# Routing of three mixture-of-experts layers on one Trainium2 core: prefix sums by scan, one-hot rows in halves on VectorE, and some work ordered behind the routing

## Chip, cores and metric

The kernel runs on one core of one Trainium2 chip. The metric is the device time of one execution in microseconds. One core has five engines that run side by side, each in its own fixed order of instructions: TensorE (PE, matmuls; its weight loads are listed as PEld), VectorE (DVE), ScalarE (ACT), GpSimd (POOL) and SyncE (SP, here used for DMA issues). They wait for each other by semaphores. The program is built by a framework whose scheduler chooses the order of each engine's instructions when the kernel is compiled, from the program order, the data dependences and a model of times; an instruction's place in the source is therefore not its place on the engine.

## The reference

The input x is 2 sequences of 1024 tokens with 128 features. Four layers follow, each of the form

```python
xn = layernorm(x)
s = mixer(xn)
g = silu(ffn(xn))
x = x + s * g
```

| layer | mixer | ffn |
|---|---|---|
| 0 | state space (Mamba 2) | 8 experts, the 2 best mixed, computed densely |
| 1 | delta rule (q, k, v, beta; a scan over tokens) | 8 experts, the 2 best, and a shared expert |
| 2 | linear attention, 16 heads | softmax attention, then 8 experts, the 2 best |
| 3 | two state spaces, one forward and one backward | 16 experts, the 2 best, and a shared expert |

The ffn of layer 1 shows what routing has to compute:

```python
logits = xf @ router_w.T + experts_bias
rw, sel = jax.lax.top_k(logits, 2)
rw = softmax(rw)
cw = (one_hot(sel, E) * rw[..., None]).sum(axis=1)
eo = silu(xf @ w1) * (xf @ w3)          # per expert
moe_out = einsum('te,teh,ehd->td', cw, eo, w2)
return moe_out + shared_out
```

## The kernel before

Tokens lie in 16 tiles of 128 (one token to a partition), in 4 groups of 4 tiles. Layers 1 to 3 do not compute every expert for every token. Each of the 2 × 2048 choices gets a slot in a list that is sorted by expert, and the list is cut into blocks of rows of one expert: 39 blocks of 128 rows in layer 1, 23 of 256 in layer 2, 47 of 128 in layer 3. A block gathers its tokens' rows (POOL, indirect DMA, `Dispatch.load`, L1231), loads its expert's weights (SP reads the expert's number from `dof` and issues a DMA, `Dispatch.weights`, L1237), runs the expert, and scatters its rows to the choices' places (POOL, `Dispatch.store`, L1241). At the end `Dispatch.fetch` (L1252) reads the two rows of each token back, and they are weighted and added.

What stands before the first block is the routing:

- `Kern.top2` (L357 to L378) finds the largest and second largest logit of each token, as two one-hot tiles (`rhot`) of 16 tiles × E experts, and the two values (`rm`).
- `Dispatch.__init__` (L1135 to L1227) adds the two one-hots (`dbo`, L1149), and two matmuls with a triangle and with ones (`pr`) give, for each expert, the number of earlier choices within the tile and the tile's total. A ladder over the 16 tiles (a copy and an addition for shifts of 1, 2, 4 and 8; L1159, L1160) makes running totals; `dmo` and `dbl` count each expert's blocks; a ladder over the experts (L1173, L1174) gives the block at which each expert ends (`de`); `dpl` is each choice's slot, and `do` and `dat` (L1185, L1186) pick it for the two choices of each token.
- The slot is split into a block row number and a place in 128 (`dhi`, `dlo`, L1188 to L1195). To turn "slot of a choice" into "choice of a slot", 32 matmuls (`pinv`, one for each tile and choice) multiply a one-hot of the place (`dla`, L1213, eight pieces of four tiles, two buffers) with a one-hot of the row, weighted with the choice's number (`dhh`: the equality on DVE at L1205, the multiply by the number on POOL at L1206). Their sum gives `dto` (L1218, where a row is scattered to) and `dfrom` (L1219, which token is gathered).
- `dpa`, `dex` and `dof` (L1223 to L1227) compare the block numbers with `de` and give each block's expert.
- `pair_softmax` (L379 to L389) makes the two weights of each token (`rd`, `rw`); its Exp runs on ACT.

What runs beside it differs by layer. In layer 1 (L786 to L1003) it is the delta rule. `delta(g, side)` inverts a triangular matrix of four tiles in seven rounds (`Lm` L909, then `pU`, a copy to `U` L284, `pTT`, `TT` L930, `pT`, `T` L937: products on PE, each answered by DVE); two groups run side by side. The program order is: the first two groups' `delta`, all blocks two by two (`block`, L791: transpose `pxb` into `xbT`, products `pgb` and `pub`, `hb` = silu times, product `pob`), four steps of `scan` (products `pWS`, `pO`, `pS`), the other two groups' `delta` (which begins with `pk`), `close`, four more steps, `close`, the shared expert (`shared`, L838: `pgt`, `put`, `po`), then `fetch` and the layer's last operations. In layer 2 (loop from L1076) it is the linear attention (`qg`, `sig`, `qk`) and the blocks (`pxb`, `p`, `po`). In layer 3 (L1722 to L1817) it is the state spaces: the step sizes start from `pdt` (L1726), go through `steps` (L436: `vdtr`, then `softplus`, L341 to L354, sixteen short operations, then `vdA`, L444), and are used by the products `pc` and, through `uda` (L556), `pd`; the matmuls `px` and `pz` belong to the state spaces too. Blocks go four by four there (`pxb`, L1771).

Every plain matmul of the program is issued at L287, inside `Kern.mm`, so the profile's rows are told apart by the names of their tiles.

Of the kernel before, what the change touches and what calls it, by code (L numbers as in the profile page):

```python
# [19 lines left out]
P = 128  # L20
# [252 lines left out]
class Kern:  # L273
# [83 lines left out]
    def top2(self, pool, lg, E):  # L357


        nc = self.nc  # L360
        big = [P, NT, E]
        rev = self.c[f"rev{E}"].unsqueeze(1).to_broadcast(big)
        cur, found = lg, []
        for n in range(2):
            t = lambda s, w: pool.tile(w, F32, name=f"r{s}{n}", tag=f"r{s}{n}")
            m, hot, at = t("m", [P, NT]), t("hot", big), t("at", [P, NT])
            nc.vector.tensor_reduce(m, cur, AX.X, ALU.max)
            nc.vector.tensor_tensor(hot, cur, m.unsqueeze(2).to_broadcast(big), ALU.is_equal)
            nc.vector.tensor_mul(hot, hot, rev)
            nc.vector.tensor_reduce(at, hot, AX.X, ALU.max)  # L370
            nc.vector.tensor_tensor(hot, hot, at.unsqueeze(2).to_broadcast(big), ALU.is_equal)
            found.append((m, hot))
            if n == 0:
                rest = pool.tile(big, F32, name="rrest", tag="rrest")
                nc.vector.scalar_tensor_tensor(rest, hot, -3e38, cur, ALU.mult, ALU.add)
                cur = rest
        return found

    def pair_softmax(self, pool, m1, m2):  # L379

        nc = self.nc
        d = pool.tile([P, NT], F32, name="rd", tag="rd")
        w = pool.tile([P, NT], F32, name="rw", tag="rw")
        nc.vector.tensor_sub(d, m2, m1)
        nc.scalar.activation(d, d, AF.Exp)
        nc.vector.tensor_scalar_add(w, d, 1.0)
        nc.vector.reciprocal(w, w)
        nc.vector.tensor_mul(d, d, w)
        return w, d  # L389
# [275 lines left out]
def layer0(K, x, xn, xT, w, e):  # L665
    nc, tc, c = K.nc, K.tc, K.c
    with ExitStack() as es:
# [49 lines left out]
        (m1, _), (m2, _) = K.top2(pf, lg, 8)  # L717
# [52 lines left out]
def layer1(K, x, xn, xT, w, inp):  # L770
    nc, tc, c = K.nc, K.tc, K.c
    four = [P, G, P]
    with ExitStack() as es:
# [7 lines left out]
        with tc.tile_pool(name="r1", bufs=1) as pr:  # L781
            (m1, h1), (m2, h2) = K.top2(pr, K.logits(pr, sf, xT, w["wr"], w["br"], 8), 8)
            d = Dispatch(K, pf, pr, sf, h1, h2, 8, P, inp["lists"])
            w12 = K.pair_softmax(pf, m1, m2)
# [220 lines left out]
def layer2(K, x, xn, xT, w, inp):  # L1005
# [3 lines left out]
    with ExitStack() as es:  # L1009
# [59 lines left out]
        with ExitStack() as e2:  # L1069
# [7 lines left out]
            with tc.tile_pool(name="r2", bufs=1) as pr:  # L1077
                (m1, h1), (m2, h2) = K.top2(pr, lg, 8)
                d = Dispatch(K, pf, pr, sf, h1, h2, 8, 2 * P, inp["lists"])
                w12 = K.pair_softmax(pf, m1, m2)  # L1080
# [48 lines left out]
class Dispatch:  # L1129
# [5 lines left out]
    def __init__(self, K, keep, pool, ps, h1, h2, E, R, lists, room=None):  # L1135
# [7 lines left out]
        big = [P, NT, E]  # L1143
        flat = lambda a: a.rearrange("p a b -> p (a b)")
        tile = lambda n, shape, dt=F32: pool.tile(shape, dt, name="d" + n, tag="d" + n)
        lt, ones, both = tile("lt", [P, P], F32R), tile("on", [P, P], F32R), tile("bo", big, F32R)
        nc.vector.tensor_copy(lt, c["lt"])
        nc.vector.tensor_copy(ones, c["ones"])
        nc.vector.tensor_add(both, h1, h2)  # L1149

        pr = ps.tile([P, 2, NT, E], F32, name="pr", tag="ps")
        K.mm(flat(pr[:, 0]), lt, flat(both))
        K.mm(flat(pr[:, 1]), ones, flat(both))
        tot = tile("to", big)
        nc.vector.tensor_copy(tot, pr[:, 1])
        cur = tot
        for n, k in enumerate((1, 2, 4, 8)):
            new = tile(f"c{n}", big)
            nc.vector.tensor_copy(new[:, :k, :], cur[:, :k, :])  # L1159
            nc.vector.tensor_add(new[:, k:, :], cur[:, k:, :], cur[:, : NT - k, :])  # L1160
            cur = new
        total = cur[:, NT - 1, :]
# [4 lines left out]
        nc.vector.tensor_tensor(more, total.unsqueeze(2).to_broadcast(shape), marks.unsqueeze(1).to_broadcast(shape), ALU.is_gt)  # L1167
        blocks = tile("bl", [P, E])
        nc.vector.tensor_reduce(blocks, more, AX.X, ALU.add)
        end, k = blocks, 1  # L1170
        while k < E:
            new = tile(f"e{k}", [P, E])
            nc.vector.tensor_copy(new[:, :k], end[:, :k])  # L1173
            nc.vector.tensor_add(new[:, k:], end[:, k:], end[:, : E - k])  # L1174
            end, k = new, 2 * k
        first = tile("fi", [P, E])
        nc.vector.tensor_sub(first, end, blocks)
        place = tile("pl", big)
        nc.vector.tensor_sub(place, cur, tot)
        nc.vector.tensor_add(place, place, pr[:, 0])  # L1180
        nc.vector.scalar_tensor_tensor(place, first.unsqueeze(1).to_broadcast(big), float(R), place, ALU.mult, ALU.add)
        at = tile("at", [P, 2, NT])
        for k, hot in enumerate((h1, h2)):
            one = tile(f"o{k}", big)
            nc.vector.tensor_mul(one, hot, place)  # L1185
            nc.vector.tensor_reduce(at[:, k, :], one, AX.X, ALU.add)  # L1186
# [11 lines left out]
        (where, tag, bufs, most), (there, its, both) = room or ((pool, "dhh", 1, T), (pool, "dla", 2))  # L1198
        per = min(2 * NT, most // wide)
        hot = []  # L1200
        for a in range(0, 2 * NT, per):
            at = slice(a, min(a + per, 2 * NT))
            shape = [P, at.stop - a, wide]
            h = where.tile(shape, F32R, name="dhh", tag=tag, bufs=bufs)
            nc.vector.tensor_tensor(h, c["count"][:, :wide].unsqueeze(1).to_broadcast(shape), digits[0][:, at].unsqueeze(2).to_broadcast(shape), ALU.is_equal)  # L1205
            nc.gpsimd.tensor_mul(h, h.bitcast(F32), c["slot"][:, at].unsqueeze(2).to_broadcast(shape))  # L1206
            hot.append(h)
        pi = ps.tile([P, wide], F32, name="pinv", tag="ps")
        some = 4
        for a in range(0, 2 * NT, some):  # L1210
            shape = [P, some, P]
            lane = there.tile(shape, F32R, name="dla", tag=its, bufs=both)
            nc.vector.tensor_tensor(lane, c["lane"].unsqueeze(1).to_broadcast(shape), digits[1][:, a : a + some].unsqueeze(2).to_broadcast(shape), ALU.is_equal)  # L1213
            for q in range(some):
                K.mm(pi, lane[:, q, :], hot[(a + q) // per][:, (a + q) % per, :], a + q == 0, a + q == 2 * NT - 1)
# [7 lines left out]
        nc.vector.tensor_tensor(past, c["count"][:, : self.n].unsqueeze(2).to_broadcast(shape), end.unsqueeze(1).to_broadcast(shape), ALU.is_ge)  # L1223
# [435 lines left out]
def layer3(K, x, xn, xT, w, inp, out):  # L1659
    nc, tc, c = K.nc, K.tc, K.c  # L1660
    four = [P, G, P]
    with ExitStack() as es:
# [59 lines left out]
        with tc.tile_pool(name="r3", bufs=1) as pr:  # L1722
            lg = pr.tile([P, NT, 16], F32, name="lg")
            nc.vector.tensor_add(lg, pl[:, :, :16], w["br"].unsqueeze(1).to_broadcast([P, NT, 16]))
            pdt = pa.tile([P, NT, 4], F32, name="pdt")
            nc.vector.tensor_mul(pdt, pl[:, :, 16:], rs.unsqueeze(2).to_broadcast([P, NT, 4]))  # L1726
            (m1, h1), (m2, h2) = K.top2(pr, lg, 16)
            d = Dispatch(K, pf, pr, sf, h1, h2, 16, P, inp["lists"], ((pa, "uxs", 4, 1536), (pa, "uda", 2)))
            w12 = K.pair_softmax(pf, m1, m2)
# [137 lines left out]
```

## Time and profile before

| what | us |
|---|---|
| four runs | 1359.48, 1359.87, 1367.20, 1368.66 |
| their median | 1363.53 |
| the profiled execution | 1365.47 |
| its span | 1363.7 |
| mean granted clock of TensorE in it | 0.886 of full speed |

Over the span PE is busy for 1135.2 us, DVE for 876.4, ACT for 634.2 and POOL for 429.8. The three routings lie at these places of the profiled execution (start of the operation named):

| | layer 1 | layer 2 | layer 3 |
|---|---|---|---|
| `dbo` (the two one-hots added) | 263.50 | 871.55 | 1149.72 |
| `dto` of L1155 (totals read from `pr`) | 266.95 | 874.03 | 1151.41 |
| `dof` (the blocks' experts) | 277.55 | 890.09 | 1159.38 |
| `dhh`, equality on DVE | 282.07 | 891.53 | 1160.90 |
| `dhh`, multiply on POOL, its duration | 2.65 | 2.95 | 3.14 |
| the two `dla` beside it, together | 3.43 | 3.75 | 3.85 |
| first `pinv` | 290.99 | 898.11 | 1165.93 |
| `dfrom` | 304.60 | 906.03 | 1175.68 |
| first gather of a block's rows | 305.81 | 907.00 | 1176.13 |
| first `pxb` | 308.67 | 909.61 | 1183.40 |

A row of the timeline has the start, the duration, the engine, the line, the operation, the tile written and the tiles read, with their sizes; in brackets stands how long the engine was idle before it, and what ended that. A row with a count holds several instructions one after the other. Rows of a table by stretches have the engines' busy time in that stretch, the granted clock and the share of the DMA engines.

### The profile page before, as it was taken

Reading aid. Unit: us, or ns where it says so; the run is one execution under the profiler, and the core shown is the slowest. Engines: PE = TensorE matmul, PEld = TensorE weight load, DVE = VectorE, ACT = ScalarE, POOL = GpSimd, SP = SyncE. Lnnn points to the kernel's source line nnn. Section 1 sums busy time; section 2 is a strip of 40 time slices with the busy share of each in tenths; the row PEclk is TensorE's granted clock in tenths of the full one; section 3 lists DMA queues with packets and bytes.
Section 4 is the critical chain, followed back from the end, with each engine's and each line's share of the span. In section 5 each row is a group of like instructions: output and inputs, shape, how many; then the busy total and the mean of one; then the engine's idle time right before and its main releaser. Section 6 shows DMA issues by size and latency. Waiting matters only on the chain. (4 is left out here: it accounts for less than half of the span.)

```text
span 1363.7 us, 19123 instructions
## 1 busy us (share of the span) xinstructions
PE 1135.2 (83%) x6813; PEld 791.6 (58%) x6813; DVE 876.4 (64%) x2169; ACT 634.2 (47%) x1051; POOL 429.8 (32%) x424
## 2 busy tenths in 40 slices
PE   5699875888899738999998998669999918799985
PEld 2367464788799415544444542347778815577664
DVE  6535534785664686677777761987766469566456
ACT  7664934404612332354555666234352316355661
POOL 0352152017555260000000000034766521467743
PEclk9798776889899957799999989869999967699997
DMA  2000003014345200000000000023344530233411
GB/s 90 0 0 1 1 0 130 8 47 139 119 127 161 62 0 0 1 1 1 1 1 16 1 9 1 8 91 102 124 125 140 151 105 24 70 86 99 77 53 47
DMA packets 49039, 75.71 MB, mean 56 GB/s; under 512 B 7335, under 2 KB 36402, under 8 KB 48688
## 3 DMA queue, kind: packets, MB, share of 16 engines
q1 hardware_dynamic: 39632, 54.30, 12.9%
q0 software_dynamic: 8448, 14.98, 4.8%
q10 hardware_dynamic: 864, 5.21, 1.1%
q8 instruction: 54, 0.88, 0.3%
q14 instruction: 41, 0.34, 0.1%
HBM read 63.95 MB, written 12.85 MB: 56 GB/s over the span
## 5 line engine op out<-in xcount | busy, mean ns | idle before, releaser
L1458 DVE TENSOR_REDUCE mx<-pm 128x1 f32<-128x512 f32 (+3 forms) x304 | 182.0, 657 | 65.1 <-PE pm L287 62.8
L1502 ACT ACTIVATE pr<-psc 128x1024 f32<-128x1024 f32 x144 | 139.7, 1022 | 94.7 <-PE psc L287 61.2
L1231 POOL DMA_INDIRECT xb<-xs,dfrom x132 | 132.1, 1000 | 122.5 <-PE pxb L808 28.7
L1241 POOL DMA_INDIRECT ys<-yb,dto x132 | 135.6, 1027 | 79.3 <-issue 30.0
L1206 POOL TENSOR_TENSOR dhh<-dhh,w_c 128x1280 fp32r<-128x1280 f32 (+2 forms) x3 | 8.7, 2915 | 473.4 <-DVE dhh L1205 473.4
L287 PE MATMUL pm<-kT,qT 32*128 32x128 f32 (+3 forms) x576 | 118.9, 365 | 16.4 <-DVE mx L1458 12.5
L287 PEld LDWEIGHTS pm<-kT,qT 32*128 32x128 f32 x576 | 69.1, 203 | 69.0 <-DVE mx L1458 49.2
L287 PE MATMUL p<-xbT,tw 128*128 128x256 f32 x368 | 101.9, 395 | 3.9 <-ACT sg L1112 2.4
L1112 ACT ACTIVATE sg<-p,tw 128x256 f32<-128x256 f32 x92 | 41.1, 474 | 97.2 <-PE p L287 91.8
L287 PE MATMUL pat<-pr,va 128*32 128x512 f32 x576 | 82.1, 637 | 0.2 <-ACT pr L1502 0.2
L293 PE MATMUL tp<-w_c,xn 128*128 128x128 f32 x64 | 19.5, 419 | 71.2 <-DVE xn L328 43.9
L287 PEld LDWEIGHTS p<-xbT,tw 128*128 128x128 f32 x368 | 64.2, 196 | 14.2 <-ACT sg L1112 3.9
L1113 DVE SCALAR_TENSOR_TENSOR hh<-p,tw,sg 128x256 f32<-128x256 f32 x92 | 42.5, 478 | 38.5 <-ACT sg L1112 32.3
L287 PE MATMUL psc<-qT,kT 32*128 32x512 f32 x288 | 63.9, 488 | 3.4 <-ACT pr L1502 3.2
L287 PEld LDWEIGHTS po<-tw,hh 128*128 128x128 f32 x368 | 54.3, 192 | 8.1 <-issue 2.2
L293 PEld LDWEIGHTS tp<-w_c,xn 128*128 128x128 f32 x64 | 11.8, 191 | 78.9 <-DVE xn L328 27.8
L287 PE MATMUL po<-tw,hh 128*128 128x128 f32 x368 | 56.1, 276 | 0.8 <-DVE hh L1113 0.4
L287 PE MATMUL psc<-mT,onesR 32*128 32x512 f32 x288 | 53.7, 413 | 0.0
L282 ACT COPY xbT<-pxb 128x256 f32<-128x256 f32 (+3 forms) x39 | 15.6, 400 | 64.8 <-PE pxb L808 45.2
L287 PEld LDWEIGHTS psc<-qT,kT 32*128 32x128 f32 x288 | 30.2, 188 | 16.5 <-ACT pr L1502 14.3
L287 PE MATMUL pd<-uda,w_c 128*128 128x512 f32 x64 | 36.5, 674 | 0.9 <-ACT usz L528 0.9
L556 POOL TENSOR_TENSOR uda<-w_c,vdA 128x512 f32<-128x512 f32 x20 | 21.1, 1066 | 50.7 <-PE pd L287 50.0
(529 smaller groups left out, 2833.2 us busy)
## 6 DMA issues: line engine op xcount, KB each, us to landing
tw<-in_rows SPq DMA_DIRECT2D x23, 836.0 KB, 4.6
tw<-in_rows SPq DMA_DIRECT2D x39, 384.0 KB, 3.3
yt<-ys SPq DMA_DIRECT2D x24, 256.0 KB, 3.3
tw<-in_rows SPq DMA_DIRECT2D x47, 128.0 KB, 2.2
xb<-xs,dfrom POOLq DMA_INDIRECT x132, 3.4
ys<-yb,dto POOLq DMA_INDIRECT x132, 2.5
xs<-xn SPq DMA_DIRECT2D x8, 256.0 KB, 2.3
w_l<-in_l ACTq DMA_DIRECT2D x1, 1890.0 KB, 11.1
```

Of the source, the lines that this page charges most:

```text
L282: self.nc.scalar.copy(out, in_)
L287: self.nc.tensor.matmul(out, lhsT=lhsT, rhs=rhs, start=start, stop=stop)
L293: self.nc.tensor.transpose(pt[:, j, :], src(g * G + j), self.c["ident"])
L556: pool.tensor_mul(da, upto.unsqueeze(1).unsqueeze(1).to_broadcast(lay), m["dA"][:, i0 + j : i0 + j + per, :].unsqueeze(3).to_broadcast(lay))
L1112: nc.scalar.activation(sg, p1[:, k - k0, :], AF.Silu, bias=t[:, 1536 + k : 1537 + k])
L1113: nc.vector.scalar_tensor_tensor(hh[:, k, :], p2[:, k - k0, :], t[:, 1540 + k : 1541 + k], sg, ALU.add, ALU.mult)
L1206: nc.gpsimd.tensor_mul(h, h.bitcast(F32), c["slot"][:, at].unsqueeze(2).to_broadcast(shape))
L1231: self.K.nc.gpsimd.indirect_dma_start(dst, None, self.xs, bass.IndirectOffsetOnAxis(self.of_token[:, n : n + 1], 0))
L1241: d = self.K.nc.gpsimd.indirect_dma_start(self.ys, bass.IndirectOffsetOnAxis(self.to[:, n : n + 1], 0), src, None, bounds_check=2 * T - 1, ...
L1458: nc.vector.tensor_reduce(mx[:, starts.index(a), g, j : j + k], tile[0][:, : k * m].rearrange("p (j m) -> p j m", m=m), AX.X, ALU.max)
L1502: K.nc.scalar.activation(pr, ps, AF.Exp, scale=scale)
```

## The change

1. `top2` keeps its two one-hots in one tile of 2 × 16 × E and returns it whole.
2. In `Dispatch.__init__` the sums are laid out with the experts outside and the tiles inside. The ladder over tiles becomes one scan over all experts' tiles (state × mask + total; the mask, `fresh`, is 0 at each expert's first tile and 1 elsewhere, written by two memsets on POOL); its data come straight from `pr`. The ladder over experts becomes a scan of 8 or 16 numbers. The triangle is now the negative of another constant, so that one addition where there were a subtraction and an addition gives the place. The two products and sums over experts become one of twice the size.
3. The one-hot rows `dhh` are written in two halves of 16 tiles; equality and multiply are both on DVE, each half just ahead (in the program's order) of the lanes that use it.
4. `behind` adds an order, without a semaphore, for the scheduler: one instruction is to stand after another of the same engine. The blocks' experts (`past`, so `dof`), the first operation of `pair_softmax` and, in layer 3, `pdt` are put behind the last `dla`.

```diff
+    def behind(self, op, first):
+        self.tc.add_manual_dep(op.ins, first.ins.name, mybir.DependencyInfo(mybir.DependencyClass.NoSync, mybir.DependencyReason.SCHED_ONLY), reason="order")
...
-    def pair_softmax(self, pool, m1, m2):
+    def pair_softmax(self, pool, m1, m2, first):
...
-        nc.vector.tensor_sub(d, m2, m1)
+        self.behind(nc.vector.tensor_sub(d, m2, m1), first)
...
-        nc.vector.tensor_copy(lt, c["lt"])
+        nc.vector.tensor_scalar_mul(less, c["ge"], -1.0)
...
-        tot = tile("to", big)
-        nc.vector.tensor_copy(tot, pr[:, 1])
-        cur = tot
-        for n, k in enumerate((1, 2, 4, 8)):
-            new = tile(f"c{n}", big)
-            nc.vector.tensor_copy(new[:, :k, :], cur[:, :k, :])
-            nc.vector.tensor_add(new[:, k:, :], cur[:, k:, :], cur[:, : NT - k, :])
-            cur = new
+        fresh = tile("fr", big)
+        nc.gpsimd.memset(fresh, 1.0)
+        nc.gpsimd.memset(fresh[:, :, 0], 0.0)
+        cur = tile("cu", big)
+        nc.vector.tensor_tensor_scan(flat(cur), flat(fresh), flat(pr[:, 0]), 0.0, ALU.mult, ALU.add)
...
-        while k < E:
-            new = tile(f"e{k}", [P, E])
-            nc.vector.tensor_copy(new[:, :k], end[:, :k])
-            nc.vector.tensor_add(new[:, k:], end[:, k:], end[:, : E - k])
-            end, k = new, 2 * k
+        nc.vector.tensor_tensor_scan(end, c["ones"][:, :E], blocks, 0.0, ALU.mult, ALU.add)
...
-        nc.vector.tensor_sub(place, cur, tot)
-        nc.vector.tensor_add(place, place, pr[:, 0])
-        nc.vector.scalar_tensor_tensor(place, first.unsqueeze(1).to_broadcast(big), float(R), place, ALU.mult, ALU.add)
-        at = tile("at", [P, 2, NT])
-        for k, hot in enumerate((h1, h2)):
-            one = tile(f"o{k}", big)
-            nc.vector.tensor_mul(one, hot, place)
-            nc.vector.tensor_reduce(at[:, k, :], one, AX.X, ALU.add)
+        nc.vector.tensor_add(place, cur, pr[:, 1])
+        nc.vector.scalar_tensor_tensor(place, first.unsqueeze(2).to_broadcast(big), float(R), place, ALU.mult, ALU.add)
+        at, one = tile("at", [P, 2, NT]), tile("o", [P, 2, NT, E])
+        nc.vector.tensor_mul(one, chosen, turned(place).unsqueeze(1).to_broadcast([P, 2, NT, E]))
+        nc.vector.tensor_reduce(at, one, AX.X, ALU.add)
...
-            nc.vector.tensor_tensor(h, c["count"][:, :wide].unsqueeze(1).to_broadcast(shape), digits[0][:, at].unsqueeze(2).to_broadcast(shape), ALU.is_equal)
-            nc.gpsimd.tensor_mul(h, h.bitcast(F32), c["slot"][:, at].unsqueeze(2).to_broadcast(shape))
...
         for a in range(0, 2 * NT, some):
+            if a % NT == 0:
+                half = slice(a, a + NT)
+                shape = [P, NT, wide]
+                h = hot[:, half]
+                nc.vector.tensor_tensor(h, c["count"][:, :wide].unsqueeze(1).to_broadcast(shape), digits[0][:, half].unsqueeze(2).to_broadcast(shape), ALU.is_equal)
+                nc.vector.tensor_mul(h, h.bitcast(F32), c["slot"][:, half].unsqueeze(2).to_broadcast(shape))
...
-        nc.vector.tensor_tensor(past, c["count"][:, : self.n].unsqueeze(2).to_broadcast(shape), end.unsqueeze(1).to_broadcast(shape), ALU.is_ge)
+        op = nc.vector.tensor_tensor(past, c["count"][:, : self.n].unsqueeze(2).to_broadcast(shape), end.unsqueeze(1).to_broadcast(shape), ALU.is_ge)
+        K.behind(op, self.last)
...
-            pdt = pa.tile([P, NT, 4], F32, name="pdt")
-            nc.vector.tensor_mul(pdt, pl[:, :, 16:], rs.unsqueeze(2).to_broadcast([P, NT, 4]))
-            (m1, h1), (m2, h2) = K.top2(pr, lg, 16)
-            d = Dispatch(K, pf, pr, sf, h1, h2, 16, P, inp["lists"], ((pa, "uxs", 4, 1536), (pa, "uda", 2)))
-            w12 = K.pair_softmax(pf, m1, m2)
+            m1, m2, hot = K.top2(pr, lg, 16)
+            d = Dispatch(K, pf, pr, sf, hot, 16, P, inp["lists"], ((pa, "uxs", 4, 1536), (pa, "uda", 2)))
+            w12 = K.pair_softmax(pf, m1, m2, d.last)
+            pdt = pa.tile([P, NT, 4], F32, name="pdt")
+            K.behind(nc.vector.tensor_mul(pdt, pl[:, :, 16:], rs.unsqueeze(2).to_broadcast([P, NT, 4])), d.last)
```

## The prediction, on record before the changed kernel ran

> **What bounds the kernel now.** I read the page's shares first (PE 83%, DVE 64%, POOL 32% of a span of 1363.7 us, so no engine is the bound throughout), then, around each of the three routings, the timeline by engine, a table of busy time by stretches, and the idle times before the first matmul that uses the routing. The chain of waits gives no single culprit (PE 10%, DVE 3%), so each layer is read by itself. Layer 0 routes in another way and runs the same operations as before: 0.
>
> Layer 1. Routing and the delta rule's first two groups share DVE, and the first stretch of the table shows who limits: DVE busy for 28.19 of 30 us, PE for 25.26.
>
> ```profile
> core 0: us, PE busy (x) PEld busy (x) DVE busy (x) ACT busy (x) POOL busy (x), PEclk, DMA share, GB/s
> 252.00:282.00 30.00, 25.26 (x197) 23.73 (x197) 28.19 (x83) 5.03 (x8) 0.00 (x0) 0.94 0.08 26
> 282.00:304.00 22.00, 17.81 (x124) 17.54 (x123) 17.16 (x23) 1.17 (x2) 2.65 (x1) 0.77 0.11 40
> 304.00:320.00 16.00, 15.10 (x130) 14.49 (x129) 6.81 (x17) 5.42 (x10) 10.26 (x11) 1.00 0.31 88
> ```
>
> In 282:304 the granted clock is 0.77. The timeline (start, duration, engine, line, operation) shows what lies under it: the two first lanes take 3.43 us where two others take 1.29, because POOL's multiply (2.65 us from 283.70) runs beside them; the delta rule's T stands behind them on DVE, and PE waits 4.19 us for it.
>
> ```profile
> 266.95 0.28 DVE L1155 COPY dto<-pr 128x128 f32<-128x128 f32 x1
> ...
> 282.07 1.48 DVE L1205 TENSOR_TENSOR dhh<-w_c,dhi 128x1280 fp32r<-128x1280 f32 x1
> 283.47 3.43 DVE L1213 TENSOR_TENSOR dla<-w_c,dlo 128x512 fp32r<-128x512 f32 x2
> 286.83 0.68 DVE L937 TENSOR_TENSOR T<-T,pT 128x512 f32<-128x512 f32 x1
> ...
> 304.60 0.18 DVE L1219 TENSOR_SCALAR dfrom<-dto 128x40 int32<-128x40 int32 x1
> ```
>
> ```profile
> 282.21 1.16 PE L287 MATMUL pU<-T,Lm 128*128 128x128 f32 x8
> 287.56 2.07 PE L287 MATMUL pU<-T,Lm 128*128 128x128 f32 x8 [4.19 <-DVE T L937]
> ...
> 449.77 1.22 PE L287 MATMUL pob<-tw,hb 128*128 128x128 f32 x4 [3.11 <-DVE hb L820]
> 450.78 1.92 PE L287 MATMUL pgt<-xT,t 128*128 128x512 f32 x2
> ```
>
> After the gap eight matmuls take 2.07 us, .23 each after the first, where others take .11: half clock. The last two lines are the layer's tail: the last block (a single one) waits 3.11 us with nothing beside it, and only then does the shared expert start, 23 us of matmuls that end the layer (x of layer 1 is done at about 481.0).
>
> Layers 2 and 3. In layer 3 PE waits 10.06 us for POOL's product. From 1176 on PE is busy for 23.73 of 24 us, then 28.73 and 28.84 of 30: the blocks and the two-direction scan fill it whatever the routing does.
>
> ```profile
> 893.40 2.95 POOL L1206 TENSOR_TENSOR dhh<-dhh,w_c 128x1472 fp32r<-128x1472 f32 x1 [379.84 <-DVE dhh L1205]
> ```
>
> ```profile
> 1165.93 1.90 PE L287 MATMUL pinv<-dhh,dla 128*128 128x48 f32 x8 [10.06 <-POOL dhh L1206]
> 1167.66 1.89 PE L287 MATMUL pc<-vdA,w_c 128*128 128x32 f32 x8
> 1169.37 5.55 PE L287 MATMUL pinv<-dhh,dla 128*128 128x48 f32 x24
> 1174.94 3.75 PE L287 MATMUL pd<-uda,w_c 128*128 128x512 f32 x4
> ```
>
> **Layer 1, up to the row list.** The compiled order of DVE is what I add up. Before, dhh starts 15.12 us after dto (266.95 to 282.07), and between them DVE also does two rounds of the delta rule. After, the ladder over tiles (four pairs of .17–.19 and .22–.28), the ladder over experts (three pairs of .17), one of two additions and a copy are gone, the experts' step is put off, and one round instead of two is left: scan .29, dmo, dpl, dbl .29 each, second scan .20, dfi .17, six 512-element operations of the delta rule at .69, dpl .30, doubled product and sum .42 each, five casts and digits .19 each. That is 7.8 us, less .08 to .10 at each of the ten seams between independent operations: 6.9. A scan is not in the trace. The nearest rows are two-input operations on 128 and 256 elements (.29, .42); a slow one is RECIPROCAL, .54 on 64 elements against .25 on 16, so .9 and 1.7 at the scans' sizes. I take the two-input row, nearest in operands; the far end costs +.6, +.6 and +1.3. top2's operations end about 1.2 us earlier in the new order (less beside them), so the scan starts at 265.2 and dhh at 272.1: 9.97 earlier.
>
> [...]
>
> The halves: 640 elements at the slope between 512 (.69) and 1280 (1.48) are .82. The order is two equalities, two lanes, Lm, multiply: 1.56 + 1.30 + .60 + .75 = 4.2, so the first pinv may start at 276.3. POOL no longer works beside the lanes, and T stands ahead of them: PE's gap shrinks from 4.19 to about 1.2, which is 3.0 us; and the half-clock spell after it (some 8 us at .50) is worth 4. Whether 1.2 us keeps the clock is bounded by two rows: gaps of .3 to 1.0 in the tail leave it whole, while one of 2.10 at 337.89 was followed by .52. I take kept; if not, +4.
>
> [...]
>
> From the first multiply to dfrom DVE has 29 operations that add up to 16.1 us (13 of .69, three pairs of lanes at 1.30, one multiply .82, dpa .49, dex .48, and small ones), less seams 14.0: dfrom at 290.3 instead of 304.60, 14.3 earlier. dpa, dex and dof now stand behind the lanes; SP's weight loads move from 278.52 to about 290, land 3.3 us later and have to be there when the first rows are transposed, at 291.2 + 2.9 = 294: no wait. If that cover goes, a landing is at most .5 late.
>
> **Layer 1, afterwards.** 14.3 is not the gain: two rounds of the delta rule, before the row list till now, come after it. A round is 48 matmuls at .111, 5.5 us of PE, or 6.4 us alone, because DVE answers each product. By PE's work alone 14.3 − 11.0 = 3.3 remain. But PE's order has two more pairs of blocks ahead of the second half's first pk (six pob instead of four), and these fill what the rounds leave idle. A pair is 3.0 us of PE (27 matmuls or transposes), a scan step beside it 1.8, and the pair's period before is 5.3. From the first pgb at 296.4 to pk I count one round and a half 8.3, six pairs 18.0, four scan steps 7.1, pW and pTV 2: 35.4, so pk at about 332, before 333.03. The remaining pairs then run at the old period, two fewer of them: the last pob ends 1 + 2 × 5.3 + about 1 = 12.6 earlier, and pgt starts at about 438. The displaced scan steps go between pgt and po, where PE waits for DVE; they cost their PE work, two pairs' worth: 1.8 to 3.6. I take −10 for the layer: 12.6 less 2.6. Bounds: −14.3 at best (all of dfrom's lead kept), −3.3 where PE's work decides, and +1 where the clock drops too.
>
> **Layer 2.** DVE is busy 21.13 of 22 us here too. Ladders −1.46, one addition −.2, dhh's phase from 5.28 (1.69 and 3.75, overlapped) to 4.6, against it the put-off dpa, dex, dof (.35, .36, .20) and two more table loads of ACT (1.28 each), because the weights' Exp now stands between sigmoids. dfrom about 1.9 earlier (906.03 to 904.2), but qk .4 later, and the first pxb stands behind pqT in PE's order: −.5. Bounds: −2 (dfrom's lead kept) to +2 (both loads exposed, less .5).
>
> **Layer 3.** dbo earlier gives nothing, as PE works on px until 1150.55; the scan starts at 1150.95. Without ladders (2.2 and 1.1 us), step sizes and experts (about 1.0 and 1.75) between, dhh starts at 1155.5, before 1160.90. Halves .9 each: 1155.5 + 1.7 + 1.3 + .85 = 1159.35 for the first pinv (−6.6), the last ends about 1167, dto 1168.1, dfrom 1168.7 (−7.0). But step sizes are now behind the last lane: softplus is 16 operations, each on the one before, .19 to .25 with one of .54, 4.5 us from 1168.4; vdA at 1173 instead of 1152.28, which before cost nothing. PE's order sets pc behind three pxb and pd behind the fourth, and the fourth gather lands about 1176.4 (1169.2 + three pitches of 1.27 + 3.4). So pd starts at about 1176.6 instead of 1174.94, with four pxb and 32 pinv already done (before, pinv too was done; the pxb, 1.0 us, came later). +.5, the clock being at half on both sides. Bounds: −2 (the pxb and a shorter half-clock spell) to +3 (the wait is all loss).
>
> POOL's two memsets per layer and the turned layout are costed at nothing: POOL was idle 71.5, 379.8 and 22.1 us before its multiply, and shapes keep their sizes. Uncovered, a memset of 128 elements would cost one short operation, .11 for 64 elements on DVE.
>
> **Sum.** −10 − .5 + .5 = −10.0. The profiled execution took 1365.47 (span 1363.7, 1.8 around it), 1.9 above the median of the four, 1363.53. It would be 1355.5; against the median 1353.5.
>
> **Rivals.** (1) PE's work decides layer 1: the rounds swallow all but 3.3, and the tail's pgt is still behind the last scan steps. For it: PE is busy 29.65 and 30.00 of 30 us at 360:390 and 390:420. Against: 304:360 and 420:482 hold 24 idle us. −3.3 − .5 + .5: 1360.2. (2) Slower: layer 3's step sizes. Softplus is late, waits among dto, dfrom and the gather's copies, and PE idles from the last pinv to pd as it did for 10.06 us before. Price if the chain takes the 9.4 us from pdt to vdA that it took before (1142.90 to 1152.28): pd at 1179, 4 late, and then half clock for the 8 to 14 us that followed the 10.06: 4 to 7. So +8 to +11, and it passes to the end, PE being full from 1176. For it: every operation of the chain waits for the last. Against: DVE has little else there. With the forecast's layer 1 it would leave 1361 to 1364; it decides once layer 1 returns less than its price: 1363.5 − 3.3 − .5 + 8 = 1367.7, with nothing returned 1371 to 1374. (3) Halving does not do what it says: both multiplies must pass before the first pinv, .75 per layer: 1355.8.
>
> **Chances.** Forecast .60, rival 1 .20, rival 2 .15, rival 3 .05. No change means within 0.5%, 6.8 us: 1356.7 to 1370.3. The forecast is nearly always below (its own range is 1349 to 1358, with .04 above 1356.7), rival 3 mostly. Rival 1 is no change, rival 2 slower with .10 of its .15. Faster .60, same .30, slower .10. The range takes in rival 1 and reaches into rival 2: 1347 to 1365.
>
> **What would show it.** L1206 gone; no dla above .8 us; PE's gap before layer 1's first pinv 1 to 2 us and the clock of the next 10 us near 1.0; dfrom at about 290, 904 and 1169 (less any shift); six pob before the second pk at about 332; pgt at 437 to 440, layer 1's x at about 471; in layer 3 pd at 1176 to 1177 relative to px's end. I am wrong if pgt moves by less than 6, if scans take over 1 us, or if pd stands over 3 us later.

## The result, and the profile after

| kernel | runs | median us | range us | ratio to the kernel before |
|---|---|---|---|---|
| before | 63 | 1365.04 | 1359.48 to 1371.74 | |
| changed | 42 | 1362.05 | 1356.42 to 1371.73 | 0.9982, 95% interval 0.9972 to 0.9991 |

The changed kernel is faster by about 2.5 us (0.18%). The forecast was 10 us. The time lies inside the stated range, the sign is right, and the gain is a quarter of what was forecast: by the measure set in the prediction this is no change.

The profiled execution of the changed kernel has a span of 1356.8 us, 6.9 less than before, and that difference must not be taken at its face. The table cuts each profile at the end of the last addition to x of each layer, in the timeline of VectorE (223.18 + 0.69 = 223.87 for layer 0 before, and so on).

| | layer 0 | layer 1 | layer 2 | layer 3 |
|---|---|---|---|---|
| before | 223.9 | 257.1 | 634.5 | 244.6 |
| changed | 219.6 | 251.2 | 633.8 | 248.6 |
| difference | −4.3 | −5.9 | −0.7 | +3.9 |

Layer 0's operations stand in the same order on PE, DVE, ACT and POOL in both kernels. POOL alone has one operation more, a memset of the mask. Its 4.3 us are chance (the last section returns to it). The other three make −2.7, near the measured 2.5. That they come so near is partly luck: two profiles of one and the same kernel (no_behind, in the experiments) differ by 3.0 us in layer 1 and 2.1 in layer 2, though only by 0.2 in layer 3. So layer 1 gave some 6 of the 10, and layer 3 took back 3.9.

Layer 1 after, from the timeline of DVE and then of PE (start, duration, engine, line, operation, idle time before it and what ended that):

```profile
262.21 0.41 DVE L1166 TENSOR_TENSOR_SCAN dcu<-dfr,pr 128x128 f32<-128x128 f32 x1
...
268.81 1.56 DVE L1203 TENSOR_TENSOR dhh<-w_c,dhi 128x640 fp32r<-128x640 f32 x2
270.29 1.29 DVE L1207 TENSOR_TENSOR dla<-w_c,dlo 128x512 fp32r<-128x512 f32 x2
...
286.32 0.18 DVE L1213 TENSOR_SCALAR dfrom<-dto 128x40 int32<-128x40 int32 x1
```

```profile
272.97 1.07 PE L287 MATMUL pinv<-dhh,dla 128*128 128x40 f32 x8 [2.14 <-DVE dhh L1204]
...
292.71 0.33 PE L813 MATMUL pxb<-w_c,xb 128*128 128x128 f32 x1 [1.49 <-DMA xb<-xs,dfrom]
...
296.30 0.39 PE L287 MATMUL pgb<-xbT,tw 128*128 128x128 f32 x2
...
332.27 1.03 PE L287 MATMUL pk<-w_l,xT 128*128 128x257 f32 x4
...
437.00 0.69 PE L287 MATMUL pob<-tw,hb 128*128 128x128 f32 x4
437.53 1.02 PE L287 MATMUL pgt<-xT,t 128*128 128x512 f32 x2
```

The lanes take 1.29 instead of 3.43, the gap before the first pinv is 2.14 instead of 4.19, and eight pinv take 1.07: the clock stays up (1.00 from 270 to 283 us). dfrom comes 66.70 us after layer 0's end instead of 80.72: 14.0 earlier. The last block waits for nothing and the shared expert follows at once. What does not fit is the stretch between dfrom and the first pgb: 10.0 us, against 6.3 before. PE is idle for only 1.9 us of it; the rest it fills with the delta rule.

The timeline of all engines around dfrom shows what is new there:

```profile
286.25 2.06 SPq L1232 DMA_DIRECT2D tw<-in_rows  x3
286.32 0.18 DVE L1213 TENSOR_SCALAR dfrom<-dto 128x40 int32<-128x40 int32 x1
...
287.44 1.16 POOL L1226 DMA_INDIRECT xb<-xs,dfrom  x1 [68.12 <-DVE Lm L914]
```

SP issues the first weights (384 KB each) in the 1.2 us ahead of the first gather and on beside it. From that gather's issue to the first pxb it takes 5.27 us; before, with the weights landed long ago, 2.86 (305.81 to 308.67). The weights are slower too, but less: the third and fourth of the burst land 5.1 and 5.3 us after their issue, where in the kernel before they took 4.7 and 4.8. In the 5.27 us the DMA engines are busy for 0.93 of the time and move 298 GB/s, in the 2.86 us before for 0.08 and 23 GB/s.

Layer 3 after, from PE's timeline and DVE's:

```profile
1151.39 7.41 PE L287 MATMUL pinv<-dhh,dla 128*128 128x48 f32 x32 [4.73 <-DVE dhh L1204]
1164.24 0.45 PE L1766 MATMUL pxb<-w_c,xb 128*128 128x128 f32 x1 [5.44 <-SPq L1231]
...
1166.77 1.75 PE L287 MATMUL pc<-vdA,w_c 128*128 128x32 f32 x8
1168.34 0.45 PE L1766 MATMUL pxb<-w_c,xb 128*128 128x128 f32 x1
1168.59 3.62 PE L287 MATMUL pd<-uda,w_c 128*128 128x512 f32 x4
```

```profile
1142.28 0.69 DVE L1166 TENSOR_TENSOR_SCAN dcu<-dfr,pr 128x256 f32<-128x256 f32 x1 [1.49 <-PE pr L287]
...
1145.01 1.03 DVE L1180 TENSOR_TENSOR do<-rhot,dpl 128x512 f32<-128x512 f32 x1
...
1160.01 0.22 DVE L343 SCALAR_TENSOR_TENSOR spe<-vdtr 128x64 f32<-128x64 f32 x1
...
1164.52 0.29 DVE L449 SCALAR_TENSOR_TENSOR vdA<-vdt,vna 128x32 f32<-128x32 f32 x2
```

PE's idle time has moved, not gone: 10.06 ahead of the first pinv before, now 4.73 ahead of it and 5.44 behind the last, where it has nothing to do until the first gathered rows land (the gather was issued 3.4 us before that pxb) and vdA is done. pd starts 63.9 us after layer 2's end (1104.67), where before it was 59.4 (1174.94 less 1115.52).

### The profile page after: what moved, and what is told of

The parts are those of the page before. It is cut to its first block, busy times and chain, and to the rows that moved or that the text cites. A ratio compares the mean times of both kernels' runs of the same rounds, so it can differ in the third digit from the quotient of the medians.

```text
span 1356.8 us, 19082 instructions
## 1 busy us (share of the span) xinstructions
PE 1128.8 (83%) x6813; PEld 786.7 (58%) x6813; DVE 874.7 (64%) x2128; ACT 631.6 (47%) x1050; POOL 421.7 (31%) x427
## 5 line engine op out<-in xcount | busy, mean ns | idle before, releaser
L287 PEld LDWEIGHTS pm<-kT,qT 32*128 32x128 f32 x576 | 69.1, 204 | 68.9 <-DVE mx L1453 49.0
L287 PE MATMUL p<-xbT,tw 128*128 128x256 f32 x368 | 98.4, 385 | 3.4 <-ACT sg L1117 3.2
L287 PE MATMUL pcum<-kv,w_c 128*128 128x512 f32 x64 | 35.8, 660 | 3.5 <-DVE prod L1317 3.1
```

The costliest lines, as they stand in the source:

```text
L287: self.nc.tensor.matmul(out, lhsT=lhsT, rhs=rhs, start=start, stop=stop)
```

## The experiments

Ten kernels, two of them measured twice, with 6 to 12 timed runs each. The layers are those of one profile each, cut as above.

| kernel | layer 0 | layer 1 | layer 2 | layer 3 | ratio (95%) |
|---|---|---|---|---|---|
| pdt_early | 219.6 | 253.1 | 635.5 | 244.2 | 0.9963 (0.9941 to 0.9984) |
| dof_free | 228.1 | 251.6 | 634.6 | 251.5 | 0.9993 (0.9973 to 1.0013) |
| pdt_dof | 223.6 | 251.5 | 633.6 | 242.5 | 0.9934 (0.9910 to 0.9958) |
| no_behind | 228.3 | 249.3 | 634.5 | 243.3 | 0.9929 (0.9904 to 0.9955) |
| no_behind_again | 219.4 | 252.3 | 632.4 | 243.5 | 0.9906 (0.9882 to 0.9931) |
| scans_alone | 217.8 | 252.7 | 640.5 | 245.6 | 0.9977 (0.9957 to 0.9998) |
| halves_alone | 217.9 | 252.5 | 634.0 | 244.1 | 0.9928 (0.9905 to 0.9951) |
| halves_again | 222.4 | 250.4 | 634.0 | 244.2 | 0.9950 (0.9932 to 0.9967) |
| whole_dve | 218.2 | 253.8 | 631.3 | 245.6 | 0.9949 (0.9926 to 0.9971) |
| halves_in_order | 220.3 | 250.8 | 632.6 | 243.7 | 0.9919 (0.9891 to 0.9947) |
| pdt_late_alone | 222.2 | 259.6 | 634.8 | 254.6 | 1.0079 (1.0053 to 1.0104) |
| dof_late_alone | 218.9 | 258.0 | 633.6 | 244.9 | 1.0003 (0.9982 to 1.0025) |

### Undoing the orders behind the lanes

**pdt_early**: the step sizes ahead of top2 again.

```diff
+            pdt = pa.tile([P, NT, 4], F32, name="pdt")
+            nc.vector.tensor_mul(pdt, pl[:, :, 16:], rs.unsqueeze(2).to_broadcast([P, NT, 4]))
             m1, m2, hot = K.top2(pr, lg, 16)
...
-            K.behind(nc.vector.tensor_mul(pdt, pl[:, :, 16:], rs.unsqueeze(2).to_broadcast([P, NT, 4])), d.last)
```

> The changed kernel with one thing undone: in layer 3 the step sizes (pdt) stand ahead of top2 again and are not ordered behind the lanes. Measured so far: from the last h of layer 2 to the last x of layer 3 took 244.7 us before and 248.6 us in the changed kernel. Theory (late step sizes hold up pc and pd): vdA ends long before the last pinv, pd starts within 2 us of the later of dfrom and px's end instead of 8 us after dfrom, layer 3 takes 243.5 to 245.5 us, ratio to before 0.994 to 0.996. Rival (the loss is the clock's phase and the half-clock pinv): pd moves, but layer 3 still takes 247.5 us or more, ratio 0.9975 to 0.999.

Layer 3 took 244.2 us, as expected, and pd started at 57.0 instead of 63.9. The busy time of 16 us of layer 3, from 60.0 us after layer 2's end, shows both halves of the price. First the changed kernel, then this one (behind the busy times of PE, PEld, DVE, ACT and POOL stand PEclk, the DMA engines' share and GB/s):

```profile
1164.70:1180.70 16.00, 14.49 (x50) 8.69 (x51) 6.08 (x12) 7.65 (x12) 9.12 (x9) 0.73 0.42 116
```

```profile
1168.10:1184.10 16.00, 15.50 (x67) 9.12 (x67) 6.17 (x11) 10.45 (x15) 10.45 (x12) 0.93 0.52 148
```

With late step sizes PE does 50 matmuls in these 16 us, with early ones 67; late, it is idle 1.0 us more, and the granted clock is 0.73 instead of 0.93. The ratio went from 0.9982 to 0.9963, just short of the expected 0.994 to 0.996; the intervals overlap, so the time alone would not settle it, the layer does.

**dof_free**: the blocks' experts no longer ordered.

```diff
-        op = nc.vector.tensor_tensor(past, ...)
-        K.behind(op, self.last)
+        nc.vector.tensor_tensor(past, ...)
```

> The changed kernel with one thing undone: the blocks' experts (past, so dof) are no longer ordered behind the last lane, in all three layers. Measured so far in layer 1: first gather issue to first pxb 2.86 us before, 5.27 us in the changed kernel, where the weight loads (4 of 384 KB) are issued at 286.25 to 289.1 and the first gather at 287.44; layer 1 (last x of layer 0 to last x of layer 1) 257.1 us before, 251.2 changed. Theory (weights and rows fight for the DMA engines): dof at least 8 us ahead of dfrom, gather to pxb 2.8 to 3.3 us, layer 1 takes 247.5 to 250 us although dhh starts about 1 us later, ratio 0.995 to 0.997. Rival (the gather is slow by itself or PE is the bound there): gather to pxb stays above 4.5 us or layer 1 takes 251 us or more, ratio 0.998 to 1.000.

The gather did as the theory has it: 2.70 us to pxb.

```profile
298.32 1.16 POOL L1225 DMA_INDIRECT xb<-xs,dfrom  x1 [70.51 <-PE pT L287]
...
301.02 0.34 PE L813 MATMUL pxb<-w_c,xb 128*128 128x128 f32 x1 [1.07 <-DMA xb<-xs,dfrom]
```

The price was not: dfrom came 69.1 us after layer 0's end instead of 66.7, since dpa, dex and dof are back in DVE's way, and layer 1 took 251.6, as with the order (251.2). The first pgb (75.3 instead of 76.7) and the second half's first pk (111.3 instead of 112.7) did come 1.4 us earlier than in the changed kernel. That lead is gone by 140 us after layer 0's end: in the 10 us before, the clock is 0.67 here and 0.83 in the changed kernel. pgt comes at 218.2, against 217.9. (Layer 3 still has its late step sizes here, 251.5.)

**pdt_dof**: both edits.

> Both undone: step sizes ahead of top2, blocks' experts free; only pair_softmax stays behind the lanes. Theory (both orders cost, in different layers): ratio 0.991 to 0.994, layer 1 248 to 250 us, layer 3 243.5 to 245.5 us. Rival (neither matters): ratio 0.998. If only one matters the ratio is that of its own run.

The ratio fell into the theory's interval, 0.9934; the gain is in layer 3 (242.5), and layer 1 stayed at 251.5, against the theory. Its lead over the changed kernel at pk, 1.6 us, goes at the same place as in dof_free, with the clock at 0.67 too.

**no_behind**: these two, and pair_softmax free as well.

```diff
-        self.behind(nc.vector.tensor_sub(d, m2, m1), first)
+        nc.vector.tensor_sub(d, m2, m1)
```

> No order behind the lanes at all: scans, merged products and halves on DVE alone. Theory (the scans and halves give the gain, the order behind them takes it back): ratio 0.991 to 0.994, as in the run with both undone; in layer 2 the two extra table loads of ACT go. Rival (the order is what shortens the way to dfrom): dfrom in layer 1 comes over 3 us later after dbo than the 26.7 us of the changed kernel, and the ratio is 0.998 or above.

Both were half right. dfrom in layer 1 did come 32.0 us after dbo instead of 26.7, as the rival has it, and the ratio was 0.9929 all the same. dbo itself stood 2.2 us earlier in this profile, so from layer 0's end dfrom is 3.1 later than in the changed kernel, and layer 1 took 1.9 less; in the second profile dfrom is 5.7 later and layer 1 took 1.1 more. A loss of layer 1 that follows dfrom does not show within the 3 us by which the two differ. (That difference stands already at dbo, 37.9 and 41.1 us after layer 0's end.) In layer 2 ACT has 24 table loads again, as before the change, instead of 26. Its layer 3 on PE's timeline, to be laid beside that of the changed kernel:

```profile
1160.40 1.90 PE L287 MATMUL pinv<-dhh,dla 128*128 128x48 f32 x8 [6.59 <-DVE dhh L1204]
1162.12 1.89 PE L287 MATMUL pc<-vdA,w_c 128*128 128x32 f32 x8
1163.83 5.55 PE L287 MATMUL pinv<-dhh,dla 128*128 128x48 f32 x24
1169.40 3.75 PE L287 MATMUL pd<-uda,w_c 128*128 128x512 f32 x4
```

pc runs among the pinv, and pd follows the last of them without a gap; neither waits for dfrom.

### Each order alone, on the kernel before

**pdt_late_alone**: pdt built after `Dispatch` and ordered behind the last lane, nothing else.

> The kernel before with one part of the change alone: layer 3's step sizes ordered behind the last lane. Theory (softplus is a serial chain that pd waits for): pd starts 63.5 to 67 us after layer 2's end instead of 59.4, later than in the changed kernel because dfrom is later too, layer 3 takes 248 to 252 us (244.6 before), layers 1 and 2 as before, ratio 1.0025 to 1.005. Rival (the chain hides behind the gather, which lands about as late): layer 3 245 us or less, ratio 0.999 to 1.001.

It cost more than expected: 1376.71 us, ratio 1.0079. pd started at 65.3, 5.9 later than before, and layer 3 took 9.9 us more. PE's timeline:

```profile
1166.76 7.41 PE L287 MATMUL pinv<-dhh,dla 128*128 128x48 f32 x32 [9.77 <-POOL dhh L1210]
1177.81 0.45 PE L1775 MATMUL pxb<-w_c,xb 128*128 128x128 f32 x1 [3.65 <-issue]
...
1180.29 1.76 PE L287 MATMUL pc<-vdA,w_c 128*128 128x32 f32 x8
1181.85 2.05 PE L287 MATMUL pd<-uda,w_c 128*128 128x512 f32 x2
```

The idle time ahead of pinv is as before (9.77), a second one follows, and in the 16 us from 60.0 us after layer 2's end (1176.6 to 1192.6) the clock is 0.65, where the kernel before has 0.87. Counted from layer 2's end, the same instructions of PE run 7.8 us later than before from 81 to 146 us; a further 2 us come after that in this one profile.

**dof_late_alone**: the blocks' experts ordered behind the last lane, nothing else.

> The kernel before with one part of the change alone: the blocks' experts ordered behind the last lane in all three layers. Theory (dfrom comes 1 to 2.5 us earlier since dpa, dex and dof leave DVE's way, but the weights then land together with the first rows): in layer 1 first gather issue to first pxb 4.5 us or more instead of 2.86, first pgb no earlier than before, layer 1 within 1 us of 257.1, ratio 0.999 to 1.002. Rival (the weights' late landing costs in each layer): layers 1 to 3 together over 4 us longer, ratio above 1.003; or (the wait is gone) under 0.998.

As the theory has it: ratio 1.0003. Layer 1's first gather and its pxb on the timeline:

```profile
295.70 2.89 SPq L1242 DMA_DIRECT2D tw<-in_rows  x4
296.94 1.16 POOL L1236 DMA_INDIRECT xb<-xs,dfrom  x1 [17.22 <-DVE T L941]
...
302.33 0.33 PE L812 MATMUL pxb<-w_c,xb 128*128 128x128 f32 x1 [2.16 <-DMA xb<-xs,dfrom]
```

5.39 us instead of 2.86. dfrom came 3.9 us earlier (76.8 after layer 0's end), the first pgb 0.9 later (87.9 against 87.0).

### Scans and halves apart

**scans_alone**: no_behind with `dhh` as it was (one equality, multiply on POOL).

> Parts 1 and 2 of the change alone (one tile of one-hots, scans, merged products), with dhh as before (one equality, multiply on POOL) and no order behind the lanes. Theory (scans shorten the way to dhh, but POOL's multiply beside two lanes still costs PE its gap and the half clock after it): dhh in layer 1 at 10.5 to 14.5 us after dbo (18.57 before, 10.7 to 14.1 in the kernels with scans so far), the two lanes beside POOL above 3 us, layer 1 takes 252 to 255 us (257.1 before, 249.3 to 251.5 with the halves), ratio 0.995 to 0.998. Rival (the halves bring nothing): layer 1 249 to 251 us and ratio 0.992 to 0.994.

0.9977, with dhh 13.5 us after dbo and layer 1 at 252.7. The lanes beside POOL cost what they did before, and PE has its gap and its half clock (sixteen pT in 3.62 us, where they take 1.95 at full clock):

```profile
273.90 3.44 DVE L1208 TENSOR_TENSOR dla<-w_c,dlo 128x512 fp32r<-128x512 f32 x2
274.08 2.71 POOL L1201 TENSOR_TENSOR dhh<-dhh,w_c 128x1280 fp32r<-128x1280 f32 x1 [56.61 <-DVE dhh L1200]
```

```profile
276.85 1.59 PE L287 MATMUL pinv<-dhh,dla 128*128 128x40 f32 x8 [1.98 <-POOL dhh L1201]
...
280.47 3.62 PE L287 MATMUL pT<-U,TT 128*128 128x128 f32 x16
```

Its layer 2 was 5 us longer than in any other profile. 4.4 us of its 6 over the kernel before are there by 177 us into the layer, long before that layer's routing, which begins at about 390; the rest was not followed up.

**halves_alone**, **halves_again**: the kernel before with part 3 alone. The one equality and POOL's multiply ahead of the loop go, and in the loop stand:

```diff
+            if a % NT == 0:
...
+                nc.vector.tensor_tensor(h, ..., ALU.is_equal)
+                nc.vector.tensor_mul(h, h.bitcast(F32), c["slot"][:, half]...)
```

> Part 3 alone: dhh in two halves, both operations on DVE; sums by ladders as before, no order behind the lanes. Theory (the halves take away POOL's multiply beside the lanes, so PE's gap of 4.19 us ahead of the first pinv in layer 1 falls under 2.5 us): first pinv in layer 1 5 to 6.5 us after dhh's start instead of 8.9, in layer 3 4 instead of 5.03, layer 1 takes 252 to 255 us, layer 3 243.5 to 244.5, ratio 0.995 to 0.998. Rival (the scans bring it all): ratio 0.999 to 1.001.

> The kernel with the halves alone once more, on the same chip as the next three. Ratio of the first time: 0.9928 (0.9905 to 0.9951). Theory (the halves bring all of the gain): 0.992 to 0.995, and within 0.002 of the kernel with scans and halves and no order. Rival (the first time was layer 0's luck, and scans and halves add up): 0.995 to 0.997, the kernel with both 0.003 below it.

0.9928 and 0.9950, the first below the expected 0.995 to 0.998. In the first profile PE's gap in layer 1 fell to 2.12 us and moved behind T alone; the first pinv came 6.8 us after dhh instead of 8.9:

```profile
281.06 2.07 PE L287 MATMUL pU<-T,Lm 128*128 128x128 f32 x8 [2.12 <-DVE T L937]
282.93 1.74 PE L287 MATMUL pTT<-TT,U 128*128 128x128 f32 x8
284.43 1.05 PE L287 MATMUL pinv<-dhh,dla 128*128 128x40 f32 x8
```

The clock was at half for the first row and most of the second (2.07 and 1.74 us, where eight take 1.16 at full clock) and full again at the third (1.05); before, half speed lasted to about 295 (granted clock 0.50 from 287 to 295 us, 1.00 from 297 to 304).

**no_behind_again**: scans, merged products and halves once more.

> Scans, merged products and halves without any order behind the lanes, once more. First time 0.9929 (0.9904 to 0.9955). Theory: 0.992 to 0.994. Rival (scans and halves add up): 0.003 or more below the kernel with the halves alone.

0.9906: on the same chip 0.0044 below the halves alone, as the rival has it; the first time, on two chips, it was 0.0001 above them. Over both times the halves bring 0.6%, both parts 0.8%. The 0.2% between them is what the scans bring alone, but it is no larger than the half-width of the intervals: whether the parts add up is not shown. Layer 1 does not show it either: 252.7 with the scans alone, 252.5 and 250.4 with the halves alone, 249.3 and 252.3 with both.

**whole_dve**: one word of the kernel before.

```diff
-            nc.gpsimd.tensor_mul(h, h.bitcast(F32), c["slot"][:, at]...)
+            nc.vector.tensor_mul(h, h.bitcast(F32), c["slot"][:, at]...)
```

> The kernel before with one word changed: the multiply of dhh on DVE instead of POOL, in one piece. It tells the two things in part 3 apart. Theory (what counts is that POOL no longer works beside the lanes): the two lanes take 1.3 us again, first pinv in layer 1 6 to 7.5 us after dhh's start (8.9 before), layer 1 252 to 255 us, ratio 0.993 to 0.996. Rival (the halves count, as the first pinv waits for half a multiply): first pinv as late as before or later, ratio 0.998 to 1.000.

0.9949, with the lanes at 1.29 again and the first pinv 5.6 us after dhh, sooner than expected:

```profile
275.37 1.48 DVE L1205 TENSOR_TENSOR dhh<-w_c,dhi 128x1280 fp32r<-128x1280 f32 x1
276.77 1.29 DVE L1213 TENSOR_TENSOR dla<-w_c,dlo 128x512 fp32r<-128x512 f32 x2
279.18 1.48 DVE L1206 TENSOR_TENSOR dhh<-dhh,w_c 128x1280 fp32r<-128x1280 f32 x1
```

```profile
278.71 1.16 PE L287 MATMUL pU<-T,Lm 128*128 128x128 f32 x8 [2.04 <-DVE T L937]
...
280.98 1.88 PE L287 MATMUL pinv<-dhh,dla 128*128 128x40 f32 x8
```

On this chip the halves had 0.9950. So the halves are worth nothing that can be measured here: what counts is that the multiply left POOL. DVE does it in 1.48 us, POOL in 2.65, and there it also stretched the lanes by 2.1 (3.43 against 1.29). Where the 0.5% is won is less clear. PE's gap is 2.04 instead of 4.19, but the half clock is still there: PEclk is 0.50 from 280 to 286, and eight pinv take 1.88 where at full clock they take 1.05. Layer 1 is 3.3 us shorter than before, and 1.6 of these stand already at 31 us, ahead of the routing; layer 3 is 0.9 longer.

**halves_in_order**: no_behind, with the second equality ordered behind the first multiply.

> Scans and halves without the order behind the lanes, with one order more: the second half's equality stands behind the first half's multiply, as the program's text has it, instead of both equalities first. Theory: the first pinv comes 0.7 to 0.9 us sooner after dhh's start in each layer than without (4.16, 4.42 and 3.95 us), which in layer 1 is worth at most 1 us and in layers 2 and 3 nothing: ratio within 0.002 of the kernel without it, not tellable apart. Rival (the wait for the first pinv sets the layers' ends): 0.002 to 0.003 lower.

The first pinv came 0.75, 0.84 and 0.86 us sooner after dhh in layers 1 to 3, and the ratio, 0.9919, lies between the two of the kernel without it.

The lowest medians are those of no_behind: 1353.48 and 1351.50 us, 0.8% below the kernel before and some 0.6% below the changed one. halves_in_order (0.9919) and pdt_dof (0.9934) cannot be told from it.

## Why the prediction was wrong, step by step

- **Layer 1, up to dfrom: right.** 66.7 us after layer 0's end against 66.4 forecast (290.3 less 223.87). The scan began 1.3 us later than forecast (42.6 against 41.3), and the steps behind it took 1.0 less than their sum. The scan takes 0.41 and 0.69 us, nearer the two-input row (0.29, 0.42) than the slow bound (0.9, 1.7). POOL's multiply and PE's 4.19 us went; the gap is 2.14 rather than 1.2, and the clock held (1.00 from 270 to 283 us).
- **Layer 1, the weights: this step failed.** "a landing is at most .5 late" was argued from the landing time of weights alone. They land beside the first gather, and both are slower together (gather to pxb 5.27 us against 2.86, the third and fourth weights 5.1 and 5.3 against 4.7 and 4.8). (Its "land 3.3 us later" equals the median of all the weight loads; in layer 1's first burst the third and fourth took 4.7 and 4.8 before.) From dfrom to the first pgb it was 10.0 us instead of 6.1, 3.9 lost. In the changed kernel's profile pk (112.7 us after layer 0's end, forecast 108.1) and pgt (217.9 against 214.1) are late by about as much, and the scan steps at the end cost 3.1 instead of 2.6: by this count that is the difference between −10 and −5.9. The cause of the slow gather is shown, by the order put in alone (2.86 to 5.39) and taken out (5.27 to 2.70). That it cost the layer 4 us is not shown: taken out, it gives 1.4 us at the first pgb and at pk, as dfrom is then later by 2.4, and nothing at pgt.
- **Layer 1, what the lead is worth: mis-sized.** "The last pob ends 12.6 earlier" was the term; the tail did shorten, and pgt came 9.0 us sooner. The changed kernel and those with orders undone have dfrom from 66.7 to 72.4 and pgt from 217.5 to 220.9, and the earliest dfrom does not have the earliest pgt. So a part of dfrom's lead is used up on the way, as the rival "PE's work decides" has it; its number (−3.3) was too small, for −5.9. What the rest consists of stays open. PE's gap and the half-clock spell after it, which the changed kernel wins back, are a candidate. The half clock alone does not explain it: scans_alone and whole_dve still have it, and their layer 1 took 252.7 and 253.8, 4.4 and 3.3 less than before.
- **Layer 2: the number right, by luck** (−0.5 forecast, −0.7 measured; one kernel's two profiles differ by 2.1 there). dfrom came 0.3 us earlier after layer 1's end instead of 1.9, and the first p is 4.9 later than before (436.8 against 431.9). The layer is no longer for it, so the first block's start did not set its end here.
- **Layer 3: the second step that failed.** "So pd starts at about 1176.6" (61.1 after layer 2's end, +1.7) was 63.9 (+4.5). The chain behind the lanes was forecast well: 4.5 us from spe to vdA, then pc, a pxb and pd. It started 2.4 us late (spe at 55.3, 52.9 forecast): dbo came at 35.5, where before it was 34.2, the scan waited for pr until 37.6 (35.4 forecast), and scan and product took 0.6 more than their rows. And "+.5, the clock being at half on both sides" set 1.2 us of work done early against it; what came back was 0.6. The clock stayed low for longer behind PE's second idle stretch: 0.73 in the 16 us from 60.0 us after layer 2's end, against 0.87 before and 0.93 in pdt_early, which waits only 0.58 us behind its last pinv.
- **The rival that came true.** "Layer 3's step sizes", given .15, named the place, the second idle stretch (5.44 us) and the half clock after it (0.50 from 1164 to 1170 us). Its price, +8 to +11, is about what the order costs alone, 7.8 to 9.9 us. In the changed kernel, where the routing is faster, it is half of that: layer 3 stands 3.9 above before and 4.3 above pdt_early. I weighed it by "DVE has little else there", which says nothing about when a serial chain may begin.
- **Halving does not do what it says**: true in part. The compiled order has both equalities first, and setting it right moves pinv by 0.75 to 0.86 us as priced; the time does not move by more than the noise (0.9919, between 0.9929 and 0.9906).
- **Costed at nothing**: the turned layout was not free. A sum of one-hots written turned takes 0.60 instead of 0.42 (256 elements), the product with turned places 1.03 on 512 elements, where the plain row has 0.69. Together that is 0.5 us in layer 3.

Together the two orders hold the missing gain: with both undone (pdt_dof) the ratio is 0.9934, some 9 us, and the forecast was 10. The share of the order of `pdt` is seen in layer 3; that of `dof` is seen at the first gather and in no layer's length.

What stays open is why the orders of `dof` and `pdt` seem to interact: freeing `dof` moved the ratio by +0.0011 with late step sizes and by −0.0029 with early ones. Both lie within the intervals. Open too is where the multiply's move to DVE wins its 0.5%, since the half clock in layer 1 stays.

## What to carry to other kernels

When a scheduling order puts work "behind" a critical step, ask what that work feeds: a serial chain of sixteen short operations at the head of the next stage needed its early start (started late, it cost layer 3 9.9 us in the kernel before) more than the step needed its 0.2 us on VectorE, and transfers moved back landed on top of those that the step released (first gather to pxb 5.39 us instead of 2.86). Test each part of a change alone: here one word (the engine of one multiply) held most of the gain, and two orders that looked harmless cancelled most of it. An earlier release need not give its whole lead (here dfrom came 14.0 us earlier, and layer 1 gave 5.9): count first what the engine that does the later work had idle or slowed.

## What the runs showed of the hardware

Layer 0, whose operations stand in one order in all these kernels, takes from 217.8 to 228.3 us in the profiles shown here, more than the change itself. In two of them (no_behind, then halves_alone) the granted clock drops at different times: it is 0.91 and 0.94 up to 120 us, 0.83 and 0.93 in the stretch below, 0.89 and 0.81 from 160 to 200 and 0.60 and 0.67 from 200 to 217. The stretch from 120 to 160 in both (PEclk is the third number from the end):

```profile
120.00:160.00 40.00, 37.83 (x137) 22.77 (x136) 24.36 (x41) 31.91 (x45) 4.91 (x5) 0.83 0.00 1
```

```profile
120.00:160.00 40.00, 35.22 (x138) 19.75 (x138) 26.30 (x44) 35.66 (x48) 6.64 (x6) 0.93 0.00 1
```

0.83 against 0.93, with the same work in the same order there. A single profile can therefore hide or feign 4 us and more, and a part's effect is read from its own layer. Even that has its noise: two profiles of one kernel agree within 0.2 us in layer 3, but differ by 2.1 to 3.0 in layer 1.

The scan took 0.41 us on 128 elements and 0.69 on 256, where a two-input operation took 0.29 and 0.42: 0.12 and 0.27 us more.
